# An attention and expert kernel on one core: the first chunk's schedule, gates and weight centering rewritten

## The chip, the core and the metric

The kernel runs on one core of one Trainium2 chip. A core has five engines with a program of their own each: TensorE (PE, matrix products; the loading of its weights is shown as PEld), VectorE (DVE), ScalarE (ACT), GpSimd (POOL) and SyncE (SP), which here issues all DMA transfers. PE writes to PSUM, which DVE and ACT read[...]. The metric is device time in microseconds (us): the median of three runs is 1064.15, from 1061.42 to 1065.45.

## What is computed

Eight sequences of 1024 tokens with 256 features pass through an attention without softmax and then through a layer of 16 experts, each with a residual and a layer norm. Cut to what matters:

```python
q, k, v = split(x @ Wqkv + bqkv)                 # 256 columns each
q -= q.mean(2);  k -= k.mean(2)                  # over the features
q2 = l2norm(q*q / ((q*q).sum(2) + 1e-7), axis=2)     # per token
k2 = l2norm(k*k / ((k*k).sum(2) + 1e-7), axis=1)     # per feature, over all tokens
kv = einsum('bnc,bnd->bcd', k2, v)               # over the 1024 tokens of a sequence
x = layernorm(x + (v + q2 @ kv / sqrt(1024)) @ Wln + bln)
sel = sigmoid(einsum('bsd,ed->bse', x, expert_sel))          # gates
scores = relu(einsum('bsd,edh->bseh', x, keys))              # 16 experts, 128 wide
x = layernorm(x + einsum('bseh,ehv,bse->bsv', scores, values, sel))
```

## The kernel before

**Numbers in halves.** To keep fp32 accuracy at the speed of the rounded fp32r type, every operand is split into a high part (a copy in fp32r) and a low part (what is left), and `passes3` (L41) makes three products of each: high x high, high x low, low x high. A product in plain fp32 takes two records for each matmul in the trace.

**Chunks.** The 8192 tokens are 16 chunks of 512; two chunks are a sequence. For each chunk `tokens_x` (L327) and `tokens_n` (L349) load x transposed and x as rows (buffers of tag `ld4`, two of them) and split them; `u_k` (L383) makes k (products `kp`, bias `bkbc`, squares, scale, split `k2h`, `k2l`) and the product `ap` of x and k2, collected in `asb`, with column sums of k2 by POOL (`sums`, L430); `u_m` (L445), once for a sequence, turns these into a matrix `mh`, `ml` (products `mc`, `pm`); `u_q` (L512) makes q2 and turns it by TensorE transposes (`qt`); `u_y` (L580) makes the residual sum after the first layer norm's centering (`yp`, halves `ych`, `ycl`) and the gates. The first layer norm's scale is folded into the gates (L632 to L654): they are computed for 16 experts on 16 partitions with 512 tokens along the lane, written to DRAM (`sel`) and read back, one row for each expert, spread to 128 partitions (`selb`, L694). `u_ffn` (L688) does one expert of one chunk: product `h` (L241), times the gate (L704), halves `sh` (ACT, L706) and `sl` (DVE, L707), and product `w` (L712), which adds up over the experts in two PSUM banks. `u_end` and `u_last` do the second layer norm and the output.

The weights are prepared on the chip: q's, k's and the output weights are centered over their rows by a DVE sum, a small DVE product, ACT for the high and DVE for the low half (`mean_of`, `centered_high`, `centered_low`, L301 to L318). The expert weights come in four groups of four (`u_weights`, L659).

**The order.** Everything is written as tasks with an engine, an estimated cost and a key (its due time in experts: 16 chunk + expert, negative before the first). `Work.order` (L112) is a planner: it plays the tasks through with these costs and, on each engine, takes the ready task of the lowest key, as long as the key is at most WINDOW = 9 ahead of the oldest task not done (AHEAD = 120 in the start) and buffers are free. Tasks with `port=True` are not laid beside one another on DVE and POOL. Each engine's program is the planned order, fixed; on the chip an engine that waits holds up all that stands behind it on that engine. DMAs are issued by SP in the planned order too. PE starts with 14 fp32 products of ones (`warm_up`, L279), then waits for data.

## Time and profile before

| quantity | value |
|---|---|
| median of 3 runs | 1064.15 us |
| time of the profiled execution | 1061.19 us |
| its span, first to last instruction | 1059.5 us |
| PE busy | 1023.7 us, 97% of the span |
| PEld, DVE, ACT, POOL busy | 81%, 67%, 51%, 33% |
| mean granted TensorE clock | 0.982 |
| share of PE in the chain that ended last | 93% |
| h, 1536 products of 128x512 | 604 us busy, 393 ns each |
| w, 1536 products of 128x512 | 485 us busy, 397 ns each |
| first kp product starts | 6.03 us |
| last yp product of chunk 0 starts | 57.26 us |
| first w product starts | 92.39 us |
| last w product starts | about 1048 us |

Products overlap on PE: the busy time of one is longer than the distance to the next. The page's row of 40 slices (26.5 us each) has PE at 7, 6, 6, 8 tenths in the first four and 9 in all others until the last; so all holes of PE lie in the first 107 us. `brow`, the biases spread over 128 partitions by one DMA, takes 5.8 us to land; the loads of `sl` and `svT` take 7.3 and 7.5; the gates' way through DRAM takes 1.6 us out and 3.3 us (median) back. On POOL a 128x512 operation takes about 1.3 us, on DVE 0.69, a cast of that size on ACT 0.58. A column of the trace that ends in "<-X" names what ended the idle time before an instruction.

### The profile page before, as it was taken

The page shows a single profiled execution, that of the slowest core. Times are in us where ns is not written, and L with a number is a line of the kernel's source. Part 1 is how long each engine was busy: PE and PEld are TensorE (multiplying, and loading weights), DVE is VectorE, ACT ScalarE, POOL GpSimd, SP SyncE. Part 2 cuts the span into 40 slices and gives each one's busy share as a digit, 9 for nine tenths or more (in the row PEclk, how much of TensorE's full clock was granted, in tenths as well). Part 3 has the DMA queues.
Part 4 walks back from the last instruction along what each step waited for, and adds up shares of the span by engine and source line. Part 5 has one row for each costly group of instructions (what it writes and reads, how often), then busy time and mean ns, then how long its engine had stood idle before and what let it go on. Part 6 is the DMA issues. An engine that isn't in the chain of part 4 may idle for free.

```text
span 1059.5 us, 14190 instructions
## 1 busy us (share of the span) xinstructions
PE 1023.7 (97%) x5080; PEld 858.9 (81%) x5080; DVE 706.0 (67%) x1234; ACT 542.4 (51%) x1139; POOL 348.7 (33%) x312
## 2 busy tenths in 40 slices
PE   7668999999999999999999999999999999999996
PEld 7557888888888888888888888888888888887885
DVE  6677858477575866658585675847666585757564
ACT  5577546355464635546454564635446463544232
POOL 4445442233334223433323343232334321103010
PEclk8788999999999999999999999999999999999999
DMA  4215413323141331424223142422314231222331
GB/s 131 80 54 176 150 52 113 88 85 115 61 131 65 109 96 53 139 69 128 64 82 122 57 133 67 131 71 80 111 60 136 66 100 60 87 85 71 120 114 36
DMA packets 63062, 99.25 MB, mean 94 GB/s; under 512 B 5776, under 2 KB 22160, under 8 KB 62992
## 3 DMA queue, kind: packets, MB, share of 16 engines
q1 hardware_dynamic: 62992, 98.35, 29.7%
q8 instruction: 40, 0.66, 0.3%
q14 instruction: 30, 0.25, 0.1%
HBM read 89.41 MB, written 8.91 MB: 93 GB/s over the span
## 4 chain that ended last, share of the span: by engine, by line
PE 93%; DVE 4%; ACT 2%; DMA 1%; issue 0%; SPq 0%; DVEq 0%; ACTq 0%
PE w L712 33%; PE h L241 33%; PE yp L241 8%; PE ap L241 5%; PE qp L241 4%; PE kp L241 4%; PE sp L241 1%; PE qt L559 1%; PE pm L241 1%; PE wv L241 1%; PE yv L241 1%; DMA brow<-bqkv 1%; PE mc L241 1%; ACT k L377 0%; DVE rs L246 0%; PE pw L241 0%
## 5 line engine op out<-in xcount | busy, mean ns | idle before, releaser
L706 ACT CAST sh<-h 128x512 fp32r<-128x512 f32 x256 | 149.3, 584 | 335.4 <-DVE h L704 331.3
L704 DVE SCALAR_TENSOR_TENSOR h<-h,selb 128x512 f32<-128x512 f32 x256 | 177.4, 694 | 132.4 <-PE h L241 132.2
L707 DVE TENSOR_TENSOR sl<-h,sh 128x512 fp32r<-128x512 f32 x256 | 175.2, 685 | 84.1 <-ACT sh L706 81.5
L241 PE MATMUL h<-ych,keyh 128*128 128x512 f32 x512 | 201.5, 394 | 0.0
L241 PE MATMUL h<-ycl,keyh 128*128 128x512 f32 x512 | 201.4, 393 | 0.0
L241 PE MATMUL h<-ych,keyl 128*128 128x512 f32 x512 | 201.4, 393 | 0.0
L712 PE MATMUL w<-sh,valh 128*128 128x512 f32 x512 | 162.7, 399 | 0.9 <-ACT sh L706 0.9
L712 PE MATMUL w<-sl,valh 128*128 128x512 f32 x512 | 161.2, 396 | 0.3 <-DVE sl L707 0.3
L712 PE MATMUL w<-sh,vall 128*128 128x512 f32 x512 | 161.0, 395 | 0.0
L724 POOL TENSOR_TENSOR w<-w,ycl 128x512 f32<-128x512 f32 x30 | 38.2, 1295 | 243.4 <-DVE w L721 243.4
L712 PEld LDWEIGHTS w<-sl,valh 128*128 128x128 f32 x512 | 95.9, 188 | 24.4 <-DVE sl L707 1.3
L712 PEld LDWEIGHTS w<-sh,vall 128*128 128x128 f32 x512 | 96.3, 188 | 22.9
L241 PEld LDWEIGHTS h<-ych,keyh 128*128 128x128 f32 x512 | 96.3, 188 | 22.3
L241 PEld LDWEIGHTS h<-ych,keyl 128*128 128x128 f32 x512 | 96.2, 188 | 22.1
L241 PEld LDWEIGHTS h<-ycl,keyh 128*128 128x128 f32 x512 | 96.3, 188 | 21.9
L712 PEld LDWEIGHTS w<-sh,valh 128*128 128x128 f32 x512 | 89.9, 189 | 15.2 <-ACT sh L706 1.3
L403 POOL TENSOR_TENSOR k<-k,ks 128x512 f32<-128x512 f32 x28 | 29.0, 1058 | 192.9 <-DVE ks L381 192.9
L608 DVE SCALAR_TENSOR_TENSOR ycl<-yp,by,ych 128x512 fp32r<-128x512 f32 x32 | 23.9, 747 | 48.7 <-ACT ysq L606 44.8
L358 POOL TENSOR_TENSOR nl<-nf,nh 128x512 fp32r<-128x512 f32 x30 | 38.1, 1292 | 51.8 <-ACT nh L355 51.8
L552 POOL TENSOR_TENSOR q<-q,qy 128x512 f32<-128x512 f32 x30 | 31.0, 1056 | 48.0 <-DVE qy L547 48.0
L241 PE MATMUL ap<-k2h,nh 128*128 128x256 f32 x128 | 38.3, 299 | 5.7 <-DVE qn L537 3.3
L431 POOL TENSOR_TENSOR k<-k 128x512 f32<-128x512 f32 x16 | 21.0, 1312 | 67.9 <-DVE qs L380 53.3
(314 smaller groups left out, 1944.7 us busy)
## 6 DMA issues: line engine op xcount, KB each, us to landing
selb<-sel SPq DMA_DIRECT2D x256, 256.0 KB, 3.3
nf<-x SPq DMA_DIRECT2D x16, 512.0 KB, 5.1
xf<-xT SPq DMA_DIRECT2D x15, 512.0 KB, 4.8
outT<-w SPq DMA_DIRECT2D x15, 512.0 KB, 3.5
kst<-keys SPq DMA_DIRECT2D x4, 512.0 KB, 4.3
vst<-values SPq DMA_DIRECT2D x4, 512.0 KB, 4.0
xf<-xT SPq DMA_DIRECT2D x2, 256.0 KB, 4.1
sel<-gr SPq DMA_DIRECT2D x16, 32.0 KB, 1.6
```

The costliest lines, as they stand in the source:

```text
L241: T.matmul(out, w, r, start=first and i == 0, stop=last and i == len(terms) - 1)
L358: add(e, c_pool(CH) if e == "G" else c_dve(CH), key + 1.5, lambda s=s: ENG[e].tensor_tensor(l[:, s], b[:, s], f(h[:, s]), ALU.subtract), r ...
L403: add(e, c_pool(CH) if e == "G" else c_dve(CH), key + 3 + g * 0.3, lambda tt=tt: ENG[e].tensor_tensor(q[:, tt, :], q[:, tt, :], along(s[:, ...
L431: G.tensor_tensor(src[:, 0:2, :], src[:, 0:2, :], src[:, 2:4, :], ALU.add)
L552: add(e, c_pool(CH) if e == "G" else c_dve(CH), key + 5.3 + 0.2 * g, lambda tt=tt: ENG[e].tensor_tensor(q[:, tt, :], q[:, tt, :], along(y[ ...
L559: T.transpose(o[:, t * P : (t + 1) * P], q[:, t, ct * P : (ct + 1) * P], ident.ap)
L608: add("V", c_dve(CH, ptr=True), k0 + 0.9, lambda t=t, jt=jt: V.scalar_tensor_tensor(yl[:, jt, :], t.ap, by[:, jt : jt + 1], f(yh[:, jt, :] ...
L704: add("V", c_dve(CH), key + 0.1, lambda: V.scalar_tensor_tensor(h.ap, h.ap, 0.0, sel[:, 0, :], ALU.max, ALU.mult), r=[h, sel], w=[h])
L706: add("S", c_act(CH, plain=True), key + 0.1, lambda: S.copy(a.ap, h.ap), r=[h], w=[a])
L707: add("V", c_dve(CH), key + 0.1, lambda: V.tensor_tensor(b.ap, h.ap, f(a.ap), ALU.subtract), r=[h, a], w=[b])
L712: T.matmul(wps[c][v].ap, w[:, e, v * P : (v + 1) * P], r.ap, start=e == 0 and i == 0, stop=e == NE - 1 and i == 2)
L724: add("G", c_pool(CH), key + 0.5, lambda v=v: G.tensor_tensor(w[:, v, :], w[:, v, :], f(ycl[c][:, v, :]), ALU.add), r=[(w, v), ycl[c]], w= ...
```

## The change

The change concerns the time before chunk 0's experts, with side effects on the plan of the whole.

- **Schedule.** A task may name several engines with a cost for each; the planner takes the one that would be done first. The second products (`w`) of chunk 0's first three experts (SOON = 3) become goals, 2.8 us apart. All tasks that a goal depends on are ranked by passes of a list schedule (`pack`) run alternately forward and backward, 24 rounds, the best kept (`sharpen`); their keys go ahead of all others. Until the goals are reached, other POOL tasks [...] wait, and other tasks leave one `att` PSUM slot free. AHEAD falls away. The DMA model allows eight transfers in flight and 0.5 us an issue.
- **Filler.** The 14 products at the start go. Wherever the plan finds PE idle before the first goal, it puts in two fp32 products of ones (0.44 us in the plan).
- **Gates of chunk 0** (`gates_first`). They are computed with 128 tokens on the partitions and 4 x 16 values along the lane: 16 products of 48 columns, 8 of one column for the sum of squares, small DVE and ACT operations, 4 transposes, then three fp32 products with `pick` that spread the rows of experts 0 to 2 to 128 partitions, and ACT copies. The 16 rows also go to DRAM, and experts 3 to 15 read them from there, behind the three copies. Chunk 0's column sum for the second layer norm is moved behind.
- **Weights.** wq and wln arrive transposed and are centered by fp32 products with `ic` (identity less 1/256), two for each of two halves. wk is centered by row sums as before, in smaller tasks.
- **Biases.** They arrive as a plain 128-row array, are split, and are added to chunk 0's and 1's k and q by one more product in each group; squares then read PSUM directly. For later chunks two products spread them.
- **Engines.** For chunks 0 and 1, low halves, the scaling of k and the column sums of k2 are DVE's (POOL did part of them); casts may go to DVE or ACT. Up to key 14 (EARLY) later chunks' POOL tasks may go to DVE or POOL.
- **Buffers.** Expert weights move from fixed buffers to slots g0 to g3, where the first chunks' tokens (g3) and the staging of group 0 (g2) live before.

```diff
+    def pack(self, part, before, rank, release):
+        free, port = {e: 0.0 for e in "TVSGD"}, {"V": 0.0, "G": 0.0}
...
+                        if any(max(now, free[o]) + t.cost[o] < now + t.cost[e] + (0.6 if o == "S" else -0.05) for o in t.eng if o != e and e != "S"):
+                            continue
+                        best = t
...
+    def sharpen(self, rounds=24):
+        part = [t for t in self.tasks if t.tail is not None]
+        inside = set(part)
+        deps = {t: [d for d in t.deps if d in inside] for t in part}
+        outs = {t: [o for o in t.outs if o in inside] for t in part}
+        late = max(-x for x in self.goals.values())
+        release = {t: late + x for t, x in self.goals.items()}
+        rank, best = {t: t.tail for t in part}, None
+        for _ in range(rounds):
+            start = self.pack(part, deps, rank, {})
+            span = max(start[t] + x for t, x in self.goals.items())
+            if best is None or span < best[0]:
+                best = span, start
+            back = self.pack(part, outs, start, release)
+            rank = {t: back[t] + min(t.cost.values()) for t in part}
+        for t in part:
+            t.key = best[1][t] - 2000
...
+        for t in reversed(self.tasks):
+            after = [o.tail for o in t.outs if o.tail is not None]
+            if after and t not in self.goals:
+                t.tail = max(after) + min(t.cost.values()) + (self.LATENCY if t.eng != "D" else 2.0)
+                t.key = -1000 - t.tail - (10 if t.eng == "D" and t.cost["D"] < 0.14 else 0)
+        self.sharpen()
...
-                limit = base + (AHEAD if base < -4 else WINDOW)
+                limit = max(base, 0) + WINDOW
...
+                        if e == "G" and first and t.tail is None and t.port[e]:
                             continue
...
+                        if e == "T" and self.idle and issued and first and now > 0.4:
+                            fill = Task()
+                            fill.eng, fill.fn, fill.news, fill.start, fill.done = e, {e: self.idle}, [], now, now + 0.44
+                            fill.cost, fill.key, fill.bufs, fill.tail = {e: 0.44}, 0, {}, None
+                            issued.append(fill)
+                            free[e] = now + 0.44
+                            heapq.heappush(events, free[e])
...
+                    if t in self.goals:
+                        self.idle = None
...
+    def high(key, h, b, n, r, w, free=True):
+        if free:
+            add("VS", {"V": c_dve(n, fast=True), "S": c_act(n, plain=True)}, key,
+                {"V": lambda: V.tensor_copy(h(), b()), "S": lambda: S.copy(h(), b())}, r=r, w=w, port={"V": True, "S": False})
+        else:
+            add("S", c_act(n, plain=True), key, lambda: S.copy(h(), b()), r=r, w=w)
+    def apply(key, out, a, b, op, n, r, w, engines="VG"):
+        fns = {e: (lambda e=e: ENG[e].tensor_tensor(out(), a(), b(), op)) for e in engines}
+        cost = {"V": c_dve(n), "G": c_pool(n)}
+        if len(engines) == 1:
+            add(engines, cost[engines], key, fns[engines], r=r, w=w, port=True)
+        else:
+            add(engines, cost, key, fns, r=r, w=w, port={"V": True, "G": True})
+    def spare(key):
+        return "VG" if key < EARLY else "G"
...
-    def warm_up(t):
-        for _ in range(WARM):
-            T.matmul(t[:, :P], ones.ap, ones.ap, start=True, stop=True)
-    warm = psum("warm", "w0")
-    add("T", 5.0, -800, lambda: warm_up(warm), r=[ones], w=[warm])
-    def stage(key, src, name):
-        b = sbuf("selb", [P, 2, D], name)
-        add("D", 1.4, key, lambda: nc.sync.dma_start(out=b.ap, in_=src), w=[b])
+    warm = psum("warm", "w1")
+    def keep_warm():
+        for _ in range(2):
+            T.matmul(warm[:, :P], ones.ap, ones.ap, start=True, stop=True)
+    add("T", 0.44, -800, keep_warm, r=[ones], w=[warm])
+    work.idle = keep_warm
...
+    def centered(name, src, key, tag):
+        t = psum(name + "_c", tag)
+        def run(k):
+            mm_group(t[:, k * D : (k + 1) * D], [(src[:, m, k * P : (k + 1) * P], ic[:, m, :]) for m in range(2)])
+        for k in range(2):
+            add("T", c_mm(D, 2, full=True), key, lambda k=k: run(k), r=[src, ic], w=[(t, k)])
+        return t
...
+            if bias is not None:
+                terms += [(rows[:, bias, :], bhl[:, 0])]
...
+            if c < 2:
+                add("T", c_mm(D, 14), key + g, lambda g=g, t=t: project(c, g, t, wkh, wkl, 1),
+                    r=x_parts(c, g) + [wkh, wkl, rows, bhl], w=[t])
+                squares(key + g + 0.7, q, g, s, t)
+                continue
...
-            G.tensor_tensor(src[:, 0:2, :], src[:, 0:2, :], src[:, 2:4, :], ALU.add)
+        def sums(i, src, at):
+            s0, s1 = (lambda: src[:, 0:2, :]), (lambda: src[:, 2:4, :])
+            t0, t1, to = (lambda: src[:, 0, :]), (lambda: src[:, 1, :]), (lambda: a[:, i, :])
+            engines = "V" if c < 2 else spare(key)
+            apply(at, s0, s0, s1, ALU.add, CH, [src], [src], engines)
             if even:
-                G.tensor_tensor(a[:, i, :], src[:, 0, :], src[:, 1, :], ALU.add)
+                apply(at, to, t0, t1, ALU.add, D, [src], [(a, i)], engines)
             else:
-                G.tensor_tensor(src[:, 0, :], src[:, 0, :], src[:, 1, :], ALU.add)
-                G.tensor_tensor(a[:, i, :], a[:, i, :], src[:, 0, :], ALU.add)
+                apply(at, t0, t0, t1, ALU.add, D, [src], [src], engines)
+                apply(at, to, to, t0, ALU.add, D, [src, (a, i)], [(a, i)], engines)
...
+    def gates_first(sq, key):
+        yh, yl = ych[0], ycl[0]
+        zt, gt = psum("zt"), psum("gt")
+        N = 4 * NE
+        zs, a = sbuf("t2", [P, 2, 4, NE], "zs"), sbuf("t2", [P, 2, 4, NE], "za")
+        v, y, b = (tiny(n) for n in ("gv", "gy", "gb"))
+        def zmm(j):
+            tk = slice(j * P, (j + 1) * P)
+            mm_group(zt[:, 64 * j : 64 * j + 48], [(u[:, k, tk], ewt[:, k, 0:48]) for k in range(2) for u in (yh, yl)])
+        def vmm(j):
+            tk = slice(j * P, (j + 1) * P)
+            mm_group(tt[:, j : j + 1], [(sq[:, k, tk], ones[:, 0:1]) for k in range(2)])
+        tt = psum("tt", "w0")
+        add("T", 1.8, key, lambda: [vmm(j) for j in range(4)], r=[sq, ones], w=[tt])
+        add("T", c_mm(48, 16), key, lambda: [zmm(j) for j in range(4)], r=[yh, yl, ewt], w=[zt])
+        zv = lambda o: zt[:, 0:256].rearrange("p (t n) -> p t n", t=4)[:, :, o : o + NE]
+        add("V", 0.17, key + 0.1, lambda: V.tensor_scalar(v.ap, tt[:, 0:4], 1.0 / D, EPS_LN, ALU.mult, ALU.add), r=[tt], w=[v])
+        add("S", 0.35, key + 0.1, lambda: S.copy(zs[:, 1], zv(32)), r=[zt], w=[(zs, 1)])
+        add("V", 0.23, key + 0.2, lambda: V.tensor_tensor(zs[:, 0], zv(0), zs[:, 1], ALU.add), r=[zt, (zs, 1)], w=[(zs, 0)])
+        def ln():
+            S.activation(y.ap, v.ap, AF.Ln, bias=c_zero.ap)
+            S.activation(y.ap, y.ap, AF.Exp, bias=c_zero.ap, scale=-0.5)
+        add("S", 0.6, key + 0.3, ln, r=[v, c_zero], w=[y])
+        def newton():
+            rsqrt_newton(v.ap, y.ap, b.ap)
+            V.tensor_tensor(zs[:, 0], zs[:, 0], along(y.ap, 4, NE), ALU.mult)
+        add("V", 0.75, key + 0.4, newton, r=[v, y, (zs, 0)], w=[b, y, (zs, 0)])
+        add("S", 0.37, key + 0.5, lambda: S.activation(zs[:, 0], zs[:, 0], AF.Exp, bias=c_zero.ap, scale=-1.0), r=[(zs, 0), c_zero], w=[(zs, 0)])
+        add("V", 0.2, key + 0.6, lambda: V.tensor_scalar(zs[:, 0], zs[:, 0], 2.0**62, 1.0, ALU.min, ALU.add), r=[(zs, 0)], w=[(zs, 0)])
+        def inverse_():
+            S.activation(a[:, 0], zs[:, 0], AF.Ln, bias=c_zero.ap)
+            S.activation(a[:, 0], a[:, 0], AF.Exp, bias=c_zero.ap, scale=-1.0)
+        add("S", 0.74, key + 0.7, inverse_, r=[(zs, 0), c_zero], w=[a])
+        def out():
+            V.tensor_tensor(zs[:, 0], zs[:, 0], a[:, 0], ALU.mult)
+            V.scalar_tensor_tensor(a[:, 1], zs[:, 0], 2.0, a[:, 0], ALU.subtract, ALU.mult, reverse0=True)
+        add("V", 0.46, key + 0.8, out, r=[(zs, 0), a], w=[(zs, 0), a])
+        def turn():
+            for j in range(4):
+                T.transpose(gt[:NE, j * P : (j + 1) * P], a[:, 1, j, :], ident.ap)
+        add("T", 0.5, key + 0.9, turn, r=[a, ident], w=[gt])
+        gs = sbuf("t2", [P, CH], "gs")
+        add("S", c_act(CH, plain=True), key + 1, lambda: S.copy(gs[:NE], gt[:NE, :]), r=[gt], w=[gs])
+        for e in range(SOON):
+            o = psum(f"gsp{e}")
+            selb[e] = u = sbuf("selb", [P, 1, CH], f"selb0_{e}")
+            add("T", c_mm(CH, full=True), key + 1.1 + e, lambda e=e, o=o: T.matmul(o.ap, pick[:NE, e, :], gs[:NE], start=True, stop=True), r=[gs, pick], w=[o])
+            soon.append(add("S", c_act(CH, plain=True), key + 1.2 + e, lambda o=o, u=u: S.copy(u[:, 0, :], o.ap), r=[o], w=[u]))
+        selt[0] = d = work.buf("dram", [NE, CH], F32, "sel0")
+        add("D", 0.2, key + 1.1, lambda: nc.sync.dma_start(out=d.ap, in_=gs[:NE]), r=[gs], w=[d])
...
+        if c == 0:
+            gates_first(sq, key + 2.3)
+            tot = colsum(sq, key + 6, f"yv{c}")
+            v1[c] = v = sbuf("v1", [P, CH], f"v1_{c}")
+            add("V", c_dve(CH), key + 8, lambda: V.tensor_scalar(v.ap, tot.ap, 1.0 / D, EPS_LN, ALU.mult, ALU.add), r=[tot], w=[v])
+            return
...
-        sel = sbuf("selb", [P, 1, CH], f"selb{c}_{e}")
-        add("D", 1.4, key - 3, lambda: nc.sync.dma_start(out=sel.ap, in_=selt[c][e : e + 1, :].partition_broadcast(P)), r=[selt[c]], w=[sel])
+        if c == 0 and e < SOON:
+            sel = selb[e]
+        else:
+            sel = sbuf("selb", [P, 1, CH], f"selb{c}_{e}")
+            add("D", 1.05, key - 3, lambda: nc.sync.dma_start(out=sel.ap, in_=selt[c][e : e + 1, :].partition_broadcast(P)), r=[selt[c]], w=[sel], after=soon if c == 0 else ())
...
+        if c == 0 and e < SOON:
+            work.goals[t] = -2.8 * e
...
+    def spread():
+        for i in range(2):
+            mm_group(pbb[:, i * D : (i + 1) * D], [(rows[:, i, :], bhl[:, 0])])
+    def bias():
+        V.tensor_copy(bqbc[:, 0, :], pbb[:, :D])
+        V.tensor_copy(bkbc[:, 0, :], pbb[:, D:])
+    add("T", c_mm(D, 2), -14, spread, r=[rows, bhl], w=[pbb])
+    add("V", c_dve(D, 2), -13, bias, r=[pbb], w=[bkbc, bqbc])
...
+    high_low(-68, centered("wq", sq, -69, "att"), wqh, wql)
```

## The prediction

> **What bounds the kernel now.** I read the stretches (busy time of each engine by window) first, then PE's waits, then the timeline of the first 107 us, and last the instruction groups by form. Columns of the stretches: the window, its length, then busy us (and instructions) of PE, PEld, DVE, ACT and POOL, the granted TensorE clock, DMA share, GB/s.

> ```profile
> 20.00:33.00 13.00, 13.00 (x98) 12.27 (x97) 9.98 (x21) 8.29 (x27) 7.62 (x10) 1.00 0.27 82
> 33.00:42.00 9.00, 5.48 (x25) 5.20 (x24) 5.32 (x11) 6.92 (x18) 7.48 (x8) 0.64 0.01 2
> 42.00:53.00 11.00, 5.72 (x28) 4.74 (x28) 6.90 (x18) 3.40 (x7) 2.93 (x3) 0.68 0.33 97
> 70.00:83.50 13.50, 2.48 (x11) 1.50 (x9) 11.51 (x16) 7.34 (x14) 6.69 (x6) 0.61 0.27 80
> 92.40:107.00 14.60, 14.34 (x63) 11.34 (x62) 12.64 (x20) 11.01 (x25) 8.12 (x6) 1.00 0.47 151
> 107.00:200.00 93.00, 93.00 (x480) 78.78 (x479) 65.94 (x120) 50.80 (x106) 36.31 (x32) 1.00 0.34 106
> ```

> From 107 us on PE is full to 1048.2 us; its only two waits there are 0.9 and 0.8 us. Then 11.3 us of tail follow. Both are untouched. So the change can only act in the first 107 us, where PE has holes and where the clock falls to 0.61 to 0.68. PE's waits of 0 to 107 us, total and times and longest:

> ```profile
> PE qt L559 <- DVE q L521: 7.3, 1, 7.3
> PE pw L241 <- ACT wlc L309: 4.5, 1, 4.5
> PE qt L559 <- DVE q2l L563: 3.6, 2, 2.2
> PE ap L241 <- DVE qn L537: 3.3, 1, 3.3
> PE ap L241 <- DVE q2l L563: 2.4, 1, 2.4
> ```

> And what a hole does to the clock (timeline: start, length):

> ```profile
> 22.61 0.28 PE L241 MATMUL ap<-k2h,nh 128*128 128x256 f32 x1
> 22.73 0.28 PE L241 MATMUL ap<-k2l,nh 128*128 128x256 f32 x1
> 36.65 0.42 PE L241 MATMUL ap<-k2l,nh 128*128 128x256 f32 x1
> 36.87 0.42 PE L241 MATMUL ap<-k2h,nl 128*128 128x256 f32 x1
> ```

> Starts lie 0.12 us apart warm and 0.21 after the 3.3 us hole. 512 columns take 0.2325 warm.

> **What those 107 us hold.** Useful work at the warm pitch: 228 matmuls of 256 columns (kp, qp, ap 72 each, pm 12) x 0.1185 = 27.0; 133 of 512 columns (h 43, yp 48, w 30, sp 8, yv 4) x 0.2325 = 30.9; pw, pb, transposes and mc about 7. Sum 65. So **42 us are lost**: 6 before the first product, some 26 in later waits, some 10 to the low clock. The forecast is: what is lost after the change?

> **The gates (L621 to L656).** The last product of yp ends at 57.7, the first w starts at 92.4: 35 us. Between lie operations on 16 partitions x 512, slowed beside POOL:

> ```profile
> 71.00 1.63 DVE L247 SCALAR_TENSOR_TENSOR gr<-rs,gr 16x512 f32<-16x512 f32 x1
> 72.67 1.63 DVE L638 TENSOR_TENSOR gr<-gr 16x512 f32<-16x512 f32 x1
> 79.92 0.67 DVE L651 TENSOR_TENSOR gr<-gr 16x512 f32<-16x512 f32 x1
> 80.63 1.68 DVE L652 SCALAR_TENSOR_TENSOR gr<-gr 16x512 f32<-16x512 f32 x1
> 44.95 0.16 DVE L246 TENSOR_TENSOR ka<-ka,ky 128x2 f32<-128x2 f32 x1
> ```

> The same form takes 0.67 with POOL still and 1.63 to 1.68 with it running. Token-major, a gate operation has 64 elements a lane, or 4. [...] the row of two elements says 0.16. So the fixed part is nearly all, yet nine small DVE operations sum to 1.8 where eight 512-wide ones took 9.3; counting by tile length misleads, since here 16 lanes become 128. The new chain: zmm 1.9, ACT copy 0.35, add 0.2, Newton 0.75, exp 0.3, DVE 0.2, Ln and Exp 0.6, DVE 0.45, transposes 0.5, copy 0.58, pick product 1, copy 0.58, some 10 hand-overs at 0.1 to 0.3. Sum about 9, then h x gate 0.69, sh 0.58, sl 0.69: first w some 13 us after yl. For the first three experts the trip through DRAM (82.3 to about 88) is gone; later experts still take it, behind these. What is late next is DVE.

> **When can the first w start?** DVE must do by then (0.69 for a 512-wide operation, 0.42 for 256): low halves of x and n of two chunks 8 x 0.69 = 5.5 (five to six of which were on POOL or waited there); k scale, k2l, inverse 6.2; k sums, moved from POOL, 4 x 0.69 + 6 x 0.42 = 5.3; weights and biases 8.5; M 4.2; q 3.9; y 1.5 and gates 1.8; expert weights 4.6; three experts 4.1. Sum 45.6, from 3.6 on: not before 49. PE must do: kp 5.7, ap 5.7, qp 2.85, pw and pb 4, pm 1.4, transposes 1.1, mc 1, yp 5.6, three h 4.2 = 31.6. New on PE: bias products 16 x 0.1185 = 1.9; centering of wl and wq, 8 fp32 matmuls at 0.5 (the wv row: 1.99 us for 4) = 4.0; spreading the biases 0.3; zmm 16 x 0.12 = 1.9; vmm, 16 records at mc's 0.12 = 1.9; transposes 0.5; three fp32 picks at twice a wv matmul = 3.0. Sum 13.5; sp(0) goes, -0.9. With the start that is 7 + 31.6 + 13.5 = 52. The chain after the second ap (asb add, al, pm, mt, mh, ml, yp, yh, yl, gates) is 22 us in which PE has about 15 to do. So I put the first w at **57**, between 49 (DVE full from its first input) and 68 (DVE at the share of 67% that it had here, 45.6/0.67).

> **Fillers.** They hold the clock and occupy PE in program order: no idle slot remains that a product ready early could use, unless another chunk's product was planned there. [...] The row here: pm at 49.27 ran at the 0.21 pitch although the hole before it was 1.4 us, after three other holes. [...] the low clock's 10 us go. At the start about 13 fillers of 4 records: 52 x 0.11 = 5.7 warm, 9.5 at the 0.183 that the old warm-up shows. First product at 6 to 9; I take 7.

> **Sum.** Lost after: 7 start + 13.5 new products + 3 of filler or idle beyond what other chunks' products use (none: 0; the chain's gaps unused: 10) = 23.5; less 0.9 for sp(0). Gain 42 - 23 = 19. At nothing: brow's slow landing (5.8 us; its consumers are now products at the end of kp), the doubled M cost in the plan (only order), and the loads on SP: about 14 issues at 0.43 to 0.5 us fit before 8 us, chunk 1's tokens no longer wait for an ld4 buffer (xf went out at 8.3, nf at 15.9), and a landing takes up to 7.5 us in that crowd, still before kp of chunk 1 is due at about 14; uncovered, a late xf moves the first w by its lateness. The gate loads of expert 3 on now wait on SP for the three copies; behind them stand kst, vst and tokens of later chunks, and weights 1 are due 11 us after the first w against a landing of 4 to 5: covered. Work of chunks 1 to 3 and weights 1 to 3 that ran before 92 now lies behind the first w: PE is full there, so it costs nothing while DVE keeps up (see rivals). 1061.2 (profiled execution) - 19 = 1042; the runs' median is 3 above the profiled one, so **1045**.

> **Rivals.**
> 1. *Fillers and plan pin PE to a late schedule* (0.16). The queue is in order; if first w comes at 68, lost rises by 11 less some 3 of other products: gain 11, 1053. For: ACT and DVE run faster than 0.58 and 0.69 back to back (0.5 and 0.6), which fillers waste. Against: the holes are DVE's anyway.
> 2. *Denser than I see* (0.12). First w at 49, other chunks' products in all gaps, lost 13: gain 30, 1034. For: POOL is free to share. Against: PE's own 52.
> 3. *Slower: DVE jams in the first chunk* (0.08). Behind the first w DVE owes 16 x 1.38 for experts plus about 45 (q of two chunks 10.4, k of two 12, y and gates 9, weights 9.7, M 4): 67 in PE's 71. Each two-input operation beside POOL may stretch by 0.96 (1.63 against 0.67). Slack 4: the gain is gone from 24 stretched operations on; at 30 it is +6, 1070. For: at 100 to 120 us DVE is already 94% busy. Against: PE stayed 99% busy there.
> 4. *The clock is not held* (in rival 1's chance): an instruction that truly waits blocks the fillers behind it.

> **Numbers.** Main case 0.64, its own range 1038 to 1051. Within 0.5% (about 5 us) is what one cannot tell from no change; part of rival 1 (0.04) lies there. Faster 0.88, same 0.04, slower 0.08. Range 1033 to 1057, leaving out rival 3 and the edges.

> **What would show it.** First w at 50 to 62 instead of 92.4; granted clock 1.00 from about 5 us to there; no wait of PE over 2 us after the start; zs and gs operations spanning under 12 us; kp's first product no later than 9. Wrong if: PE waits over 1 us for sl or h appear between 60 and 130 (DVE jam); fillers stand directly before products whose inputs were long there (rival 1); PE has waits beyond 130 (the new plan hurt the steady part).

## The result, and the profile after

Four runs of the changed kernel have a median of **1053.26 us** (1052.12 to 1054.82), beside 1062.82 (1061.42 to 1065.45) for the kernel before on the same chip: ratio **0.9908, 95% interval 0.988 to 0.9936**. The profiled execution took 1052.12 us, its span is 1050.4. So the change gains 9.1 us in the spans and 9.6 in the medians, where 19 were forecast. The time lies in the forecast direction and in the outer range, 1033 to 1057, but 2 us outside the main case's own, 1038 to 1051; the size is off by a factor of two.

The stretches of the changed kernel, as in the fence of before (window, length, busy us and instructions of PE, PEld, DVE, ACT and POOL, granted clock, DMA share, GB/s):

```profile
20.00:33.00 13.00, 13.00 (x102) 12.66 (x101) 11.40 (x24) 9.84 (x21) 0.00 (x0) 1.00 0.03 8
33.00:42.00 9.00, 9.00 (x68) 8.41 (x68) 8.65 (x28) 7.41 (x22) 0.00 (x0) 1.00 0.00 0
42.00:53.00 11.00, 11.00 (x88) 10.46 (x86) 8.80 (x21) 6.92 (x15) 0.00 (x0) 1.00 0.50 144
60.00:70.00 10.00, 10.00 (x56) 8.07 (x56) 9.46 (x21) 6.67 (x14) 0.00 (x0) 0.83 0.58 161
70.00:83.50 13.50, 13.50 (x70) 11.32 (x70) 10.10 (x21) 7.36 (x17) 1.28 (x1) 1.00 0.41 137
107.00:200.00 93.00, 93.00 (x467) 77.97 (x467) 63.09 (x112) 45.80 (x100) 31.55 (x27) 1.00 0.33 100
```

PE is full in every stretch, and PE's waits from 0 to 130 us are a single line, ahead of the first filler:

```profile
PE warm L411 <- POOL ones L399: 1.1, 1, 1.1
```

A page without waits does not mean a page without loss: fillers count as busy. What PE did before the first `w`, from its timeline (start, length):

```profile
40.30 2.84 PE L411 MATMUL warm<-ones 128*128 128x128 f32 x24
...
43.42 2.40 PE L411 MATMUL warm<-ones 128*128 128x128 f32 x20
...
60.66 0.60 PE L800 MATMUL gt<-ident,za 128*16 128x128 f32 x4
61.09 1.50 PE L411 MATMUL warm<-ones 128*128 128x128 f32 x12
62.52 2.84 PE L808 MATMUL gsp<-gs,pick 16*128 16x512 f32 x6
65.29 1.26 PE L411 MATMUL warm<-ones 128*128 128x128 f32 x8
66.35 1.91 PE L726 MATMUL qt<-ident,q 128*128 128x128 f32 x8
68.06 2.70 PE L411 MATMUL warm<-ones 128*128 128x128 f32 x16
70.51 0.80 PE L954 MATMUL w<-sh,valh 128*128 128x512 f32 x2
```

The first `w` starts at **70.5**, against 92.4 before and 57 in the forecast. There are 152 filler records: 64 at the start and 88 later, which took 10.6 us (0.12 each; eight of them stand at 48.4, between the last `yp` product of chunk 0 and a `qp` product). Three times the next step of the chain to the first `w` stood ready behind them or other products: the first product of `yp` at 45.6 behind the second row of 20 fillers, though its `q2h` was there at 41.4 and `mh` before; `za`, which `gt` turns, was written by 58.2, and `gt` runs at 60.7 behind products of `h`, `yv` and another chunk's `kp`; `sl` of the first expert was ready at about 67.6, and `w` runs at 70.5 behind `qt` and 16 fillers. The gates themselves became what the diff says; their DVE operations on 16x512, of which all but one took 0.67 to 1.68 us, are now 0.15 to 0.23, and the nine of them sum to 1.73, for the 1.8 of the prediction (DVE's timeline; on 4 elements a lane such an operation took 0.15 to 0.16):

```profile
55.75 0.22 DVE L780 TENSOR_TENSOR zs<-zs,gy 128x64 f32<-128x64 f32 x1
...
57.99 0.23 DVE L794 SCALAR_TENSOR_TENSOR za<-zs,za 128x64 f32<-128x64 f32 x1
```

**The account on PE's side.** Before, 42 us were lost by the first 107 us. After: start 10.0 (kp begins at 9.98), late fillers 10.6, the new products 12.2 (bias terms 1.9, `wq` and `wl` 3.3, bias spread 0.3, `tt` 1.7, `zt` 1.8, `gt` 0.4, `gsp` 2.8), about 1.5 for the low clock of 66 to 70 us (granted 0.57), less 0.9 for `sp` of chunk 0. Sum 33, so a gain of 9: what the spans show.

### The profile page after: what moved, and what is told of

Its sections match the earlier page's. It is cut to its first block, busy times and chain, and to the rows that moved or that the text cites. A ratio compares the mean times of both kernels' runs of the same rounds, so it can differ in the third digit from the quotient of the medians.

```text
span 1050.4 us, 14564 instructions
## 1 busy us (share of the span) xinstructions
PE 1039.6 (99%) x5276; PEld 874.9 (83%) x5276; DVE 713.7 (68%) x1277; ACT 542.1 (52%) x1140; POOL 302.9 (29%) x271
## 4 chain that ended last, share of the span: by engine, by line
PE 98%; DVE 1%; ACT 0%; issue 0%; POOL 0%; DVEq 0%; ACTq 0%; POOLq 0%
PE w L954 34%; PE h L347 34%; PE yp L347 9%; PE qp L347 4%; PE kp L347 4%; PE ap L347 4%; PE warm L411 2%; PE qt L726 1%; PE sp L347 1%; PE pm L347 1%; PE wv L347 1%; PE yv L347 1%; PE mc L347 1%; PE gsp L808 0%; PE pb L347 0%; PE zt L347 0%
## 5 line engine op out<-in xcount | busy, mean ns | idle before, releaser
L365 POOL TENSOR_TENSOR k<-k,ks 128x512 f32<-128x512 f32 x26 | 26.5, 1042 | 208.2 <-DVE ks L537 192.0
L841 DVE SCALAR_TENSOR_TENSOR ycl<-yp,by,ych 128x512 fp32r<-128x512 f32 x32 | 23.9, 747 | 45.6 <-ACT ysq L839 45.5
L365 POOL TENSOR_TENSOR q<-q,qy 128x512 f32<-128x512 f32 x27 | 27.6, 1042 | 48.4 <-DVE qy L714 45.2
L839 ACT ACTIVATE ysq<-yp,by 128x512 f32<-128x512 f32 x32 | 21.9, 686 | 36.6 <-PE yp L347 36.5
L695 ACT ACTIVATE qj<-q,c_zero,qs 128x256 f32<-128x256 f32 x64 | 38.0, 595 | 1.6 <-DVE qs L537 0.5
L365 POOL TENSOR_TENSOR nl<-nf,nh 128x512 fp32r<-128x512 f32 x24 | 33.6, 1423 | 16.1 <-ACT nh L361 16.1
```

What stands on the lines that cost most here:

```text
L365: fns = {e: (lambda e=e: ENG[e].tensor_tensor(out(), a(), b(), op)) for e in engines}
L695: S.activation(junk[:, t % 2 * D : (t % 2 + 1) * D], q[:, t, :], AF.Square, bias=c_zero.ap, scale=s[:, t : t + 1], accum_out=n2[:, t : t + 1])
L839: add("S", c_act(CH), k0 + 0.8, lambda t=t, jt=jt: S.activation(sq[:, jt, :], t.ap, AF.Square, bias=by[:, jt : jt + 1]), r=[t, by], w=[(sq ...
L841: add("V", c_dve(CH, ptr=True), k0 + 0.9, lambda t=t, jt=jt: V.scalar_tensor_tensor(yl[:, jt, :], t.ap, by[:, jt : jt + 1], f(yh[:, jt, :] ...
```

## Experiments

Each ratio is to the kernel before on the same chip, with its 95% interval; us are medians. The theory that the trace suggests is rival 1 of the prediction: fillers hold PE where a product could run. Its rival is that the fillers stand in real holes and pay for themselves by the clock.

**no_late_fill**: the plan is the same to the last instruction, but the fillers behind the first product are not issued.

```diff
+            if t.eng == "T" and t.fn["T"] is keep_warm:
+                fills += 1
+                if products:
+                    continue
+            elif t.eng == "T":
+                products += 1
```

> The changed kernel with its plan and every engine's order kept, but the 22 fillers (88 products of ones) behind the first real product are not issued; the 16 at the start stay. Theory P (fillers pin TensorE to a plan whose costs are too long): the 11.6 us they take are mostly not waits for data, so the first w comes at 65 to 68 instead of 70.5, the clock stays at 1.00 for most of the stretch, and the time falls by 2 to 5 us against the changed kernel, to some 1048 to 1051. Theory C (the holes are VectorE's and the fillers buy the clock): the same holes come back as waits, the granted clock falls to 0.5 to 0.7 in them, and the time rises by 2 to 5 us, to 1055 to 1058.

1050.31 us, 0.9866 (0.9851 to 0.9881). Faster than the changed kernel by 3 us in the medians and 4.5 in the ratios (the intervals just touch), not by 10. First `w` at 66.4. Its waits on PE up to 130 us, and three of its stretches:

```profile
PE qt L726 <- DVE q2l L730: 2.3, 1, 2.3
PE warm L411 <- POOL ones L399: 1.1, 1, 1.1
PE gsp L808 <- ACT gs L804: 0.7, 1, 0.7
PE w L954 <- ACT sh L948: 0.6, 1, 0.6
```

```profile
40.00:50.00 10.00, 7.71 (x43) 6.46 (x41) 9.12 (x20) 7.51 (x13) 0.00 (x0) 0.83 0.35 108
50.00:60.00 10.00, 10.00 (x55) 8.73 (x56) 6.02 (x21) 8.11 (x26) 0.00 (x0) 0.83 0.17 51
60.00:70.00 10.00, 8.71 (x34) 5.71 (x34) 9.90 (x22) 6.33 (x14) 0.00 (x0) 0.84 0.55 153
```

Of 10.6 us of fillers, 3.6 stood in waits that are there without them (2.3 + 0.7 + 0.6). The clock now falls to half three times, for about 3.4 us each, where the changed kernel has one such stretch; two more of them, 6.9 us at half the work (the `h` products stand 0.43 us apart in them, 0.23 outside), are some 3.4 us that the fillers had bought. What is left of the 10.6, 3.6 us by this estimate, they cost, which lies between the medians and the ratios. Both theories hold in part, and the balance of the late fillers is negative.

**short_start_no_late**: the same, and 8 instead of 16 filler tasks at the start (`if products or fills > 8`).

> As the run without late fillers, and at the start only 8 fillers (32 products of ones) instead of 16 (64), all orders kept. The last low half of x that the first kp products read is there at 8.0 us in the changed kernel, and kp starts at 10.0. Theory P: kp starts at about 8, and 1.5 to 2 us come on top of the run without late fillers: 1046 to 1049. Theory C: with the clock opened at about 5 us and a hole of 2 us, kp starts at 8 but part of it runs at the low clock, and nothing is won: the same as without late fillers within 1 us.

1047.51 us, 0.9842 (0.9828 to 0.9856): 2.8 us more (the intervals overlap a little; the times, 1046.09 to 1048.73 for 1048.48 to 1051.42, hardly do). kp begins at 7.1 instead of 9.98, waits twice, for 0.3 us on `wkl` and 0.2 on `xl`, and runs without a gap from 8.4; first `w` comes at 64.0. The first half of `xl`, which kp needs, was there at 8.0 in the changed kernel too. The plan counts 7.0 us for the 16 filler tasks (0.44 each), and their 64 records took 8.9 (the windows of the changed kernel hold 7 of them in each us up to 5.0 and 11 in the next, at a granted clock that reads 1.00 throughout); a filler can't be called back.

**old_gates**: the changed kernel with the old gates of 16 partitions, through DRAM, ranked anew.

```diff
-        if c == 0:
-            gates_first(sq, key + 2.3)
...
-        if c == 0 and e < SOON:
-            sel = selb[e]
-        else:
+        if True:
```

> The changed kernel with chunk 0's gates made as in the kernel before (16 partitions, through DRAM for all experts), the schedule ranked anew for that. It sizes the gates. By the prediction's row the old chain takes 35 us from the last yp product to the first w where the new one takes about 22: first w at 78 to 85, with some 8 to 12 us more of fillers or waits, so the time is 1060 to 1065, no better than before. Rival: while the gates are made TensorE has other chunks' products, and the new gates save 3 us or less net of their own 7 us of products: 1050 to 1055.

1052.14 us, 0.9884 (0.987 to 0.9897): with the new gates 0.988 to 0.9936, so no difference that shows. The hole that the old gates leave is one row of PE's timeline, ahead of the first `w`:

```profile
63.18 9.99 PE L411 MATMUL warm<-ones 128*128 128x128 f32 x88
72.93 0.80 PE L946 MATMUL w<-sh,valh 128*128 128x512 f32 x2
```

First `w` is 2.4 us later. This kernel does 60 filler records more than the changed one (212 for 152), 7 us at 0.12, and the new gates' own products (`tt`, `zt`, `gt`, `gsp`, less `sp`) are 6: what PE no longer waits, it multiplies.

**before_fill**: the kernel before, with fillers wherever its plan has PE idle up to the first `w`, and nothing else of the change.

```diff
+                        if e == "T" and self.idle and issued and now > 0.4:
+                            fill.fn, fill.news = self.idle, []
+                            issued.append(fill)
+                            free[e] = now + 0.44
```

> The kernel before with nothing of the change but the fillers: two products of ones wherever its own plan finds TensorE idle before chunk 0's first w, instead of the 14 at the start. The prediction put the low clock's loss at some 10 us of the 42. If fillers alone give that back, the time falls by 5 to 10 us to 1053 to 1058; if they pin TensorE to the plan as theory P says of the changed kernel, they eat what they save: 1060 to 1066.

1063.98 us, 0.9998 (0.999 to 1.0006), with 12 runs. The clock is held for most of the time (0.996 over the span, for 0.978 to 0.982 in the runs of before), and PE looks full or nearly so, as two of its stretches show beside those of before (0.68 and 0.61):

```profile
42.00:53.00 11.00, 8.60 (x61) 8.13 (x61) 9.55 (x12) 5.83 (x20) 6.51 (x6) 0.91 0.24 64
70.00:83.50 13.50, 13.50 (x73) 11.53 (x72) 12.39 (x22) 9.97 (x22) 5.39 (x5) 1.00 0.14 46
```

The time is the same: what the clock gives, the fillers' own time takes. There are 336 filler records, 68 of them ahead of kp, which begins at 11.3 instead of 6.03; so the start alone loses 5 us here, and what the later fillers would give without it was not tried. First `w` comes at 96.6 instead of 92.4.

**rank_only**: the kernel before with the new planner (goals, ranks, 24 rounds), no fillers, its tasks as they were.

> The kernel before with its own tasks (old gates, old centering, old biases, old engines, 14 products of ones at the start, no fillers), planned by the changed planner with the three goals and the 24 rounds. Theory R (the ranking is what gains): the first w comes at 75 to 82 instead of 92.4 and most of the 12 us between the two kernels is there: 1051 to 1057. Theory W (the work put in another form, bias products, TensorE centering, DVE for POOL, shortens the chain, and the order only follows): 1060 to 1066.

1073.32 us, 1.0089 (1.0073 to 1.0104): **slower**. First `w` is early, at 78.1, but it stands behind one wait of PE, in its waits up to 130 us:

```profile
PE w L817 <- ACT sh L811: 14.7, 1, 14.7
```

A rank that hurries a goal empties PE around it: `w` comes 14 us earlier, and by the ratio the kernel takes 9.5 us longer. That the other chunks' products, which had lain beside the old gates, now stand behind them is argued from this wait; no run tried it apart.

**parts_old_order**: all the changed tasks, but the old order of keys: no goals, no ranks, no late fillers, and the old number of products at the start.

```diff
-        self.sharpen()
+        for t in self.tasks:
+            t.tail = None
...
-                limit = max(base, 0) + WINDOW
+                limit = base + (AHEAD if base < -4 else WINDOW)
...
+    add("T", 5.0, -800, lambda: [keep_warm() for _ in range(7)], r=[ones], w=[warm])
```

> The changed kernel's tasks (new gates, centering, biases, engines) in the order that the old keys give: no goals, no ranking, no fillers behind the 14 products at the start. Theory R: without the ranking the new tasks gain little or lose by their 13 us of added products: 1060 to 1068. Theory W: 1050 to 1056. If both this and the ranking alone give about half, the two add up.

1055.12 us, 0.9922 (0.9904 to 0.994). Without any ranking the tasks alone give 8 of the gain; the whole change (0.988 to 0.9936) can't be told from it. The ranks do work with these tasks: no_late_fill, which has them and no late fillers, lies below it with an interval apart, by 6 us, though its start is longer (64 filler records for 28). The late fillers then give 4.5 of the 6 back.

**no_rounds**: ranks by the length of the chain alone, without the 24 passes (`self.sharpen()` left out).

> The changed kernel without the 24 forward and backward passes: tasks that the goals need still go first, by the length of the chain behind them. If the passes matter, the first w comes later than 70.5 by some us and the time is 1055 to 1060; if the chain length alone orders well enough, 1052 to 1054. At the start 21 fillers instead of 16 say that its plan begins later.

1056.8 us, 0.993 (0.9915 to 0.9944). The intervals overlap, so the 2 to 3 us by which it is slower are not shown; kp begins at 12.9 here, behind 84 filler records, 2.9 us later than in the changed kernel.

**center_dve**: wq and wln centered as wk is, by row sums on DVE.

```diff
-    cl = centered("wl", sl, -80, "h")
+    ml_ = mean_of(-80, sl)
...
-    high_low(-68, centered("wq", sq, -69, "att"), wqh, wql)
+    centered_rows(-69, sq, wqh, wql)
```

> The changed kernel with wq and wln centered by DVE sums and ACT, as before, instead of by 8 fp32 products (3.7 us measured), planned anew. By theory P TensorE is the queue that everything stands in until the first w, so 3.7 us fewer products give up to 3 us: 1049 to 1052. If DVE is the bound of that stretch, its added 2.5 us make it 1053 to 1056.

1053.51 us, 0.9902 (0.9887 to 0.9916): no difference. One stretch of it shows why:

```profile
20.00:30.00 10.00, 10.00 (x89) 10.00 (x88) 9.93 (x23) 6.59 (x12) 0.00 (x0) 1.00 0.01 2
```

DVE is full there (9.93 of 10, against 8.72 in the changed kernel), and PE does 48 filler records from 17.3 to 22.8 where the changed kernel centers the weights (3.3 us) and goes on. PE's time is given either to the centering or to fillers that wait for DVE's.

**wide_small**: as short_start_no_late, with the same products in the same order, but wider: `tt` of 64 columns for 1, `zt` of 128 for 48, and `pick` and `gs` filled with zeros to 128 rows from 16.

```diff
-            mm_group(zt[:, 64 * j : 64 * j + 48], [(u[:, k, tk], ewt[:, k, 0:48]) for k in range(2) for u in (yh, yl)])
+            mm_group(zt[:, P * j : P * (j + 1)], [(u[:, k, tk], ewt[:, k, :]) for k in range(2) for u in (yh, yl)])
-            mm_group(tt[:, j : j + 1], [(sq[:, k, tk], ones[:, 0:1]) for k in range(2)])
+            mm_group(tt[:, 64 * j : 64 * (j + 1)], [(sq[:, k, tk], ones[:, 0:64]) for k in range(2)])
...
-            T.matmul(o.ap, pick[:NE, e, :], gs[:NE], ...)
+            T.matmul(o.ap, pick[:, e, :], gs.ap, ...)
```

> As the run with a short start and no late fillers, all orders kept, but the three kinds of small products of the new gates are made wide at the same count: tt 64 columns of ones instead of 1, zt 128 columns instead of 48, the picks with 128 rows (112 of them zeros) instead of 16. In that run the clock stood at 0.5 for 3.4 us twice, at 50.4 to 53.8 behind tt and zt and at 63.9 to 67.3 behind the picks, while TensorE was busy. Theory A (the clock follows how much of the array works, so such products count as idle): both low stretches go, each worth some 1.6 us, and the time falls from 1047.5 to about 1044.5. Theory H (the holes of 2.3, 0.7 and 0.6 us alone lower the clock): both stay, 1047 to 1048.

1044.46 us, 0.9818 (0.9804 to 0.9832): 3 us faster in the medians and 2.6 in the ratios, though it multiplies more (1044.08 to 1044.71, for 1046.09 to 1048.73). The stretches behind these products, first of short_start_no_late:

```profile
50.00:54.00 4.00, 4.00 (x15) 3.37 (x15) 2.75 (x11) 3.97 (x15) 0.00 (x0) 0.57 0.00 0
...
64.00:67.00 3.00, 2.98 (x7) 2.40 (x8) 3.00 (x5) 1.92 (x4) 0.00 (x0) 0.50 1.10 324
```

and of wide_small:

```profile
50.00:54.00 4.00, 4.00 (x25) 3.47 (x25) 3.00 (x10) 3.97 (x14) 0.00 (x0) 1.00 0.00 0
...
64.00:67.00 3.00, 3.00 (x14) 2.44 (x13) 3.00 (x6) 1.94 (x3) 0.08 (x1) 1.00 1.09 349
```

PE is full in both kernels, yet the first works at half the clock (15 matmuls for 25, and 7 for 14). The `gsp` products last 2.84 us with 16 rows and with 128, `tt` 2.08 with 1 column and 1.89 with 64, and the `zt` products stand 0.11 us apart with 48 columns and with 128, so the wide form costs nothing that shows. One low stretch is there that the other run does not have, at 41.4 to 44.8 us behind the hole of 2.3 us, so the holes have a part in the clock too (short_start_no_late has 1.00 in this window):

```profile
40.00:50.00 10.00, 8.97 (x53) 7.85 (x53) 8.97 (x21) 6.72 (x15) 0.00 (x0) 0.83 0.52 157
```

**best**: wide_small with five late filler tasks (20 records) put back, in the one hole of over 1 us (`if late > 5 or not products and fills > 8`).

> As the run with wide small products, and in the one hole of 2.3 us (before the second qt) 5 fillers of the changed plan put back; all other late fillers stay out. If the hole still lowers the clock behind it, 0.5 to 1.5 us are won: 1043 to 1044. If the clock is held already, nothing is won and a filler that runs into its product costs 0.3: 1044.5 to 1045.

1043.78 us, 0.9812 (0.9798 to 0.9826). First `w` at 62.0, clock 0.998; 0.7 us from wide_small, which the intervals do not tell apart, but in the trace the low stretch behind the hole is gone, as the first theory had it. It beats the changed kernel by about 10 us and the kernel before by 20, by the ratios. Its waits of PE up to 130 us, behind the 1.1 at the start, are 0.8, 0.7, 0.4 and 0.2 us.

**parts_old_gates**: parts_old_order with the old gates (the diff of old_gates).

> The run with the changed tasks in the order of the old keys, but chunk 0's gates made as before (16 partitions, DRAM). That run had the first w at 71.7 and 1055.1. If the gates are worth here what the prediction gave them (a chain of 35 us against 22), the first w comes at 82 to 88 and the time is 1062 to 1066, which leaves next to nothing to the biases, the centering and the engines. If these parts gain, and other products fill the old chain as they did in the ranked plan, 1055 to 1059.

1053.42 us, 0.9904 (0.9886 to 0.9922), and first `w` at 77.0. In the old order, too, the new gates bring nothing: the intervals overlap, and the median is lower without them.

**parts_old_gates_pool**: the same, with chunk 0's and 1's operations on the engines that they had before.

```diff
-        if free:
+        if False:
...
-                          CH, [b, h], [(l, k)], "V" if c < 2 else spare(key))
+                          CH, [b, h], [(l, k)], "V" if c < 1 else "G")
...
-            engines = "V" if c < 2 else spare(key)
+            engines = "G"
```

> The kernel of parts_old_gates (all the change's parts but the gates, in the old order of keys, no goals, no late fillers), with the engines of chunks 0 and 1 as in the kernel before: POOL makes the low halves of chunk 1 and of group 0's keys and the column sums of k2, ACT alone makes the casts. Left of the change: biases by products with squares read from PSUM, centering by TensorE, buffers g0 to g3, smaller tasks, the DMA model, tasks from key -1 to 14 free to go to DVE. parts_old_gates took 1053.4, the kernel before 1062.8. Theory E (the move from POOL to DVE and the free casts are where the gain sits: an operation of 1.3 us on POOL becomes 0.69, and casts no longer queue on ACT): first w at 82 us or later, 1058 to 1063. Theory F (the biases, buffers and splitting are it): first w at 76 to 79, 1051 to 1056. Between: both.

1057.86 us, 0.9942 (0.9921 to 0.9963), and first `w` at 81.8: between the two theories. The engines are worth about 4 us, and what is left (bias products, centering by TensorE, buffers, smaller tasks, the DMA model, tasks up to key 14 free to go to DVE) about 6. Of these only the centering was tried alone, in the ranked plan, without a difference; which of the others gains stays open.

**The ladder**, in us of 1064 from the ratios: bias products, buffers, smaller tasks and the rest of that list −6; DVE for POOL and free casts −4; new gates 0 (+2 by the medians); goals and ranks −6; late fillers +4.5; sum −10, as the change shows. Beyond it: short start (from no_late_fill) −2.6, wide products −2.6, a few fillers −0.6. The steps of the first row are differences of ratios whose intervals are 3 to 4 us wide.

## Why the prediction was right in direction and half in size

- **The place** was right: the gain is all before 107 us. PE stays full from there on, and only two waits of 0.9 and 0.8 us remain near the end.
- **The new products** were priced at 13.5 and measured 12.2. Among them the fp32 products `gsp`, of 512 columns, took 0.92 us each, where the fp32r products of `h`, of the same size, stand 0.23 apart.
- **The step that failed** is in the sum: "3 of filler or idle beyond what other chunks' products use". It measured 10.6 us of late fillers. Their cost was taken as the time of true gaps, since a filler stands only where the plan has PE idle; but the plan's costs are not the chip's. Without the fillers only 3.6 us of waits showed. The start adds to it in the same way: 7 was forecast, from 13 fillers, and 10.0 came, with 16. Together these terms are 10.6 us too small, less 1.3 for the products, and the low clock, put at nothing, took about 1.5: some 11, for the 10 that are missing. The runs agree with it: with the late fillers out and the start halved 17 of the 19 us came, and 20 in best, which has the wide products too.
- **The first w at 57** came at 70.5. The 22 us counted from the sum of both `ap` to the first `w` took 40 (30.9 to 70.5): 9 to `ml`, 5.4 to `yp`, while PE ran 44 fillers (q's first low half stood 0.7 us on DVE behind `nl` and `xl` of later work, the second transposes waited for it, and `yp` stood behind 20 of the fillers), 5 for `yp` and `yl`, 14 from `yl` to the first row of gates in place of 9, and 6 to `w`. Adding up durations and hand-overs left out the queues: an operation that is ready waits its planned turn. The kernel before has this too: ACT stood idle for 3.28 and 1.80 us ahead of `gr` at 74.34 and 76.86, while the cast to `k2h` at 79.18, whose `k` POOL had written by 70.43, stood behind.
- **The gates** were given a long passage as if their 35 us were the loss. PE had work of other chunks for most of that time (it was busy for some 24 of the 35); the loss was only what PE lacked. Both tests of the old gates show an exchange of PE's waiting for PE's products at no profit that shows.
- **The low clock's 10 us "go"** was wrong as a gain: before_fill recovers most of the clock (0.996 for 0.978 to 0.982) and not one us, for the fillers there take the time that the clock saves. The row of `pm` (the 0.21 pitch behind a hole of 1.4 us and three others) raised the question which holes lower the clock, and not what filling costs.
- **Rival 1** named the mechanism and the time (1053). Its sign was right: fillers did stand before products whose inputs were there. Its size was larger in the trace (10.6 us of fillers) than in the run without them (3 us), since without the fillers 3.6 us came back as waits and some 3.4 as low clock. The chance of 0.16 was too small: what the prediction named as its sign came true, and that the outer range holds the time is owed to this rival, not to the main case.
- **Rival 3** did not happen: DVE was 95 to 96% full in the windows 33 to 42 and 60 to 70 us, but no wait for `sl` or `h` over 1 us followed, since PE had later chunks' products. **Rival 2**'s time (1034) was not reached by any version; the best one still loses about 7 at the start, 12 to the new products, 2.4 to fillers and 2.1 in waits.

## What to carry to other kernels

A product put in to keep the clock is part of the program's order and takes its time whether the hole is there on the chip or only in the plan (here 10.6 us of late fillers, for 3.6 us of waits without them): put it where the chip shows a wait, count it as lost time, and test the kernel with the fillers left out and the order kept. A short chain is worth only what PE lacks while it runs (the new gates brought nothing that shows, though the first `w` came 2.4 us earlier with them), so ask what PE does meanwhile before shortening it. Where a stretch is full and slow (here 4.00 us of 4 busy, at a clock of 0.57), look at the granted clock and at how many rows and columns the products just before it have (here 1 and 48 columns).

## What the runs showed of the hardware that was not expected

Where the low stretches begin says more. In one profile they begin multiples of about 3.42 us apart (61.5 us is 18 of them, 23.9 is 7, 13.7 is 4): at 11.5, 35.4, 45.7 and 73.0 us in the kernel before, at 42.8, 53.1 and 66.7 in no_late_fill, at 50.2 and 63.9 in short_start_no_late. If that is more than chance, what counts is what fell into the one interval of 3.4 us ahead, and these cases agree. `tt` and `zt` filled such an interval in short_start_no_late (46.8 to 50.2) and the clock fell; in the changed kernel they lay across two (1.5 us in one, 2.0 in the next), and it stayed at 1.00 from 54 to 60 us. The hole of 2.3 us lay within one in wide_small (38.0 to 41.4), and the clock fell; in short_start_no_late it was parted between two, and the clock stayed. The narrow `gsp` took 2.5 us of one in the changed kernel (62.8 to 66.2), with fillers behind it and no hole, and the clock fell; the wide `gsp` took 2.7 us of one in wide_small (58.5 to 61.9), and it stayed. So, by this reading, the gain of the wide form is not an accident of where the intervals fell. This is the author's reading of the profiles; how much of an interval must be idle or narrow was not measured, and no run moved the products against the intervals.
